# A stack of graph layers on one Trainium2 core: other filler at the start, other closing norms at the end

## The chip, the cores and the metric

The kernel runs on one core of a Trainium2 chip. A core has TensorE (PE in the profile: matrix products and transposes, written to PSUM, eight banks of 128 x 512 f32), VectorE (DVE), ScalarE (ACT), GpSimd (POOL) and SyncE (SP), which issues most DMAs. Each engine works through its own list in order; semaphores order the engines among each other. The metric is the device time of one execution in microseconds, the median of several.

## What is computed

x is 64 batches of 256 nodes with 128 channels, adj is one 256 x 256 matrix for all batches. Four layers follow, each of the form x = layernorm(x + layer(x)):

```python
def layer0(x): # X_k = adj^k x, k = 1..3, the same adj given twice
    return concat([x, X1, X2, X3, X1, X2, X3]) @ weight_1
def layer1(x): return adj @ (x @ weight) + bias
def layer2(x): # A_hat = adj + I, d = rowsum(A_hat)^-0.5
    return (d[:, None] * A_hat * d[None, :]) @ x @ W.T + b
def layer3(h): # five steps
    m = adj @ h                      # in_matrix and out_matrix are both adj
    av = concat([m, m])
    u3 = h @ u3_w.T + u3_b
    z = sigmoid(av @ w3_w.T + w3_b + u3)
    r = sigmoid(av @ w4_w.T + w4_b + u3)
    hv = tanh(av @ w5_w.T + w5_b + (r * h) @ u5_w.T + u5_b)
    h = (1 - z) * h + z * hv
```

The last norm is that of y + h, where y is the input of layer 3 and h its state after five steps.

## The kernel before

Everything is f32. The 64 batches are cut into 32 groups of two (NB = 2); a group is a tile of 128 x 512, four blocks (q) of 128 columns. `Group.record` (L879) doesn't issue instructions: it records operations with their engine, an estimated cost and lag, and what they read and write. `Plan.attempt` (L102) is a list scheduler: it takes, over all engines, the operation that can start earliest by the estimates; among operations that can start equally early on an engine it prefers those that open no new PSUM bank, then the lower `place`, which is the group's rank with a random addition. `Plan.order` (L85) makes 12 such attempts and keeps the one with the shortest estimated end. The instructions are then issued in the order of the estimated starts. So a changed estimate changes the order of the instructions on every engine, the DMA queue of SP among them, but no estimate makes anything wait: only data, buffers and the order on each engine do.

Groups from G - LEVEL = 25 on share nearly one rank, so they advance side by side. A group may start when the group twelve before it has ended (ACTIVE); the load of x of a group from the fifth on waits for the first operation of the group two before it (`load_gate`, L975).

**Start.** PE runs WARM = 12 transposes of `ident` into a spare bank (`warming`, L268). `turned_early` (L285) transposes adj into the bank `p_at` (four transposes) and adds four more idle ones; `halved` (L290) copies the bank to `aT`, one half by ScalarE, one by VectorE. `square` (L297) forms adj times adj in the bank `p_a2`, followed by two idle transposes, and `halved` copies it to `a2T`. VectorE then makes sums of blocks (`block_sums`, L380) and the summed, centred weights of layer 0 (`w0_sums` and `centre`, L312 to L327, from `w0_raw`, loaded at L308). The first three groups (HEAD) turn their x on PE (`transposes`, L815, the bank `ptx`) and multiply it by a2T directly (`pmq`); later groups have x turned by VectorE (`tx`, L889) with a trip through DRAM (`dx`, `xT`), and propagate with seven block products in place of eight (`seven`, L742). The estimates for the loads of the first four groups stand at L881.

**Middle.** A norm of layers 0 to 2 is `spread_of` (L539: ScalarE squares with a running sum, four blocks one after the other as one planned operation; GpSimd raises to the power -0.5) and a scaling on ScalarE (`normalise_centred`). The weights are centred beforehand, so that the mean is zero. In layer 3 a step is `propagate`, two gates from the bank `pr` and the bank `ph`, and VectorE's d = hv - h, e = z d, h + e. The state is kept transposed (`hT`) and brought into natural layout for the next step through DRAM.

**End.** For groups before B - END (29 of them) the last h goes through DRAM into natural layout (`hn`), is added to y, and is normalised from statistics (`statistics`, `normalise`). The last three groups (END = 6 batches) use `closing` (L706): ScalarE copies hT in another order (`hc`); PE adds, in one bank `s3`, hc turned and centred by `less` (identity minus 1/128), y by a product with `ident`, and, when it is there, e turned and centred. Then comes `spread_of`, or for the very last group `spread_at_once` (L555: the statistics by VectorE instead), a scaling by VectorE and one store.

The costs and lags of the estimates are in ns; `pe`, `dve` and `act` (L501 to L508) add the lag to hand over.

## Time and profile before

| | us |
|---|---|
| median of three runs (lowest, highest) | 1335.65 (1334.96, 1336.24) |
| the profiled execution | 1335.43 |
| its span | 1333.5 |
| PE busy | 1321.0 |
| VectorE busy | 1037.3 |
| ScalarE busy | 774.3 |
| GpSimd busy | 632.7 |

The span is the time from the first to the last instruction that the profiler saw on the core; the profiled execution's own time is 1.9 us longer. Busy times of the engines overlap each other. PE and PEld are the products and the loading of their stationary operand. In the page's groups, `s<-less,hc 128*128 128x128` names the tile written, the stationary and the moving operand, and their shapes; every f32 product shows two records, a transpose one. DMA lines of SP show the issue; the landing is told apart. Idle time in brackets behind an instruction is that of its engine just before it, with what ended it.

The rows of the page that cost most are the gates' products on PE:

```profile
L219 PE MATMUL pr<-mg,w435u5T 128*128 128x512 f32 x640 | 321.9, 593 | 0.0
...
L219 PE MATMUL ph<-mg,w435u5T 128*128 128x512 f32 x320 | 163.4, 593 | 0.0
L219 PE MATMUL pr<-hT,w2u3T 128*128 128x512 f32 x320 | 163.0, 592 | 0.0
L219 PE MATMUL ph<-rh,w435u5T 128*128 128x512 f32 x320 | 162.7, 592 | 0.0
```

They run beside each other's loading and overlap by their modelled ends, so that 593 ns of one is more than the spacing of two.

### The profile page before, as it was taken

The page shows a single profiled execution, that of the slowest core. Times are in us where ns is not written, and L with a number is a line of the kernel's source. Part 1 is how long each engine was busy: PE and PEld are TensorE (multiplying, and loading weights), DVE is VectorE, ACT ScalarE, POOL GpSimd, SP SyncE. Part 2 cuts the span into 40 slices and gives each one's busy share as a digit, 9 for nine tenths or more (in the row PEclk, how much of TensorE's full clock was granted, in tenths as well). Part 3 has the DMA queues.
Part 4 walks back from the last instruction along what each step waited for, and adds up shares of the span by engine and source line. Part 5 has one row for each costly group of instructions (what it writes and reads, how often), then busy time and mean ns, then how long its engine had stood idle before and what let it go on. Part 6 is the DMA issues. An engine that isn't in the chain of part 4 may idle for free.

```text
span 1333.5 us, 23248 instructions
## 1 busy us (share of the span) xinstructions
PE 1321.0 (99%) x6901; PEld 925.1 (69%) x6901; DVE 1037.3 (78%) x2574; ACT 774.3 (58%) x2355; POOL 632.7 (47%) x995
## 2 busy tenths in 40 slices
PE   9899999999999999999999999999999999999997
PEld 8887766766666677768677666667677786566554
DVE  6866677978788788796787788878877688777777
ACT  4576654566464664655566655645565787444445
POOL 4885642545352654455446633523444675222212
PEclk9999999999999999999999999999999999999999
DMA  7411343634454444332432443635342134344433
GB/s 185 122 53 43 82 93 90 154 91 107 115 127 111 104 118 105 102 97 73 103 98 78 111 119 106 145 83 125 81 103 64 45 106 116 92 111 93 91 86 103
DMA packets 403276, 134.38 MB, mean 101 GB/s; under 512 B 309808, under 2 KB 374960, under 8 KB 403152
## 3 DMA queue, kind: packets, MB, share of 16 engines
q1 hardware_dynamic: 402896, 132.78, 39.5%
q8 instruction: 55, 0.90, 0.3%
q0 software_dynamic: 256, 0.13, 0.2%
q14 instruction: 69, 0.57, 0.1%
HBM read 67.05 MB, written 65.54 MB: 99 GB/s over the span
## 4 chain that ended last, share of the span: by engine, by line
PE 96%; DVE 3%; DMA 1%; ACT 0%; issue 0%; POOL 0%; POOLq 0%; DVEq 0%; ACTq 0%; SPq 0%
PE pr L219 31%; PE ph L219 20%; PE pmg L219 19%; PE py L219 11%; PE pm L219 7%; PE pz L219 4%; PE pmq L219 3%; DMA x<-in_x_dram 1%; PE s L219 1%; DVE tx L890 0%; PE warm L270 0%; ACT y L545 0%; DVE se L660 0%; DVE sf L663 0%; DVE sd L654 0%
## 5 line engine op out<-in xcount | busy, mean ns | idle before, releaser
L219 PE MATMUL pr<-mg,w435u5T 128*128 128x512 f32 x640 | 321.9, 593 | 0.0
L763 POOL TENSOR_TENSOR tsg<-h 128x256 f32<-128x256 f32 x128 | 94.0, 735 | 286.9 <-DMA h<-dh 195.0
L549 POOL TENSOR_TENSOR rs<-ve,half 128x4 f32<-128x4 f32 x98 | 101.1, 1031 | 170.0 <-ACT y L545 167.5
L869 ACT ACTIVATE pr<-pr,bsum 128x512 f32<-128x512 f32 x160 | 105.5, 659 | 125.1 <-PE pr L219 124.8
L876 DVE TENSOR_TENSOR d<-ph,hT 128x512 f32<-128x512 f32 x160 | 109.6, 686 | 79.4 <-ACT ph L869 73.9
L869 ACT ACTIVATE r<-pr,bsum 128x512 f32<-128x512 f32 x160 | 105.3, 658 | 108.3 <-PE pr L219 100.0
L545 ACT ACTIVATE y<-s,root 128x128 f32<-128x128 f32 x392 | 152.2, 391 | 24.1 <-DVE s L584 22.1
L219 PE MATMUL ph<-mg,w435u5T 128*128 128x512 f32 x320 | 163.4, 593 | 0.0
L219 PE MATMUL pr<-hT,w2u3T 128*128 128x512 f32 x320 | 163.0, 592 | 0.0
L219 PE MATMUL ph<-rh,w435u5T 128*128 128x512 f32 x320 | 162.7, 592 | 0.0
L219 PEld LDWEIGHTS pr<-mg,w435u5T 128*128 128x128 f32 x640 | 107.7, 191 | 63.5 <-issue 47.9
L869 ACT ACTIVATE ph<-ph,bsum 128x512 f32<-128x512 f32 x160 | 105.3, 659 | 72.3 <-PE ph L219 71.7
L876 DVE TENSOR_TENSOR rh<-r,hT 128x512 f32<-128x512 f32 x160 | 109.2, 683 | 30.8 <-ACT r L869 29.6
L219 PEld LDWEIGHTS pmg<-aTp,h 128*128 128x128 f32 x512 | 86.7, 191 | 60.7 <-issue 38.4
L577 ACT ACTIVATE y<-s,rs 128x128 f32<-128x128 f32 x384 | 122.1, 393 | 7.1 <-POOL rs L549 6.9
L876 DVE TENSOR_TENSOR pr<-pr,d 128x512 f32<-128x512 f32 x157 | 108.2, 691 | 1.1
L876 DVE TENSOR_TENSOR hT<-hT,pr 128x512 f32<-128x512 f32 x157 | 106.2, 678 | 1.8
L219 PE MATMUL pmg<-s_aTp,tsg 128*128 128x128 f32 x768 | 106.7, 275 | 0.0
L910 POOL TENSOR_TENSOR yb<-y,wb 128x512 f32<-128x512 f32 x64 | 82.4, 1288 | 41.1 <-ACT y L577 40.8
L219 PEld LDWEIGHTS ph<-rh,w435u5T 128*128 128x128 f32 x320 | 58.0, 190 | 57.6 <-issue 45.6
L219 PEld LDWEIGHTS pmg<-s_aTp,tsg 128*128 128x128 f32 x768 | 96.0, 192 | 0.0
L219 PE MATMUL pmg<-aTp,h 128*128 128x128 f32 x512 | 95.7, 274 | 0.0
(206 smaller groups left out, 2784.7 us busy)
## 6 DMA issues: line engine op xcount, KB each, us to landing
dh<-th SPq DMA_DIRECT2D x160, 256.0 KB, 2.1
h<-dh SPq DMA_DIRECT2D x512, 64.0 KB, 2.4
x<-in_x_dram SPq DMA_DIRECT2D x32, 256.0 KB, 3.2
hT<-dh SPq DMA_DIRECT2D x128, 64.0 KB, 2.0
out_dram<-y SPq DMA_DIRECT2D x32, 256.0 KB, 2.4
dx<-tx SPq DMA_DIRECT2D x29, 256.0 KB, 2.4
xT<-dx SPq DMA_DIRECT2D x58, 128.0 KB, 2.7
dn<-tn SPq DMA_DIRECT2D x29, 256.0 KB, 2.0
```

The lines of the kernel that those rows point to most:

```text
L219: nc.tensor.matmul(o, lhsT, rhs, start=start, stop=stop, skip_group_check=shared)
L545: nc.scalar.activation(nat(y)[:, q, :], nat(s)[:, q, :], AF.Square, scale=C ** -0.5, bias=root[:, 0:1], accum_out=ve.ap[:, q:q + 1])
L549: nc.gpsimd.tensor_tensor(rs.ap, ve.ap, half[:, :self.q], op=OP.pow)
L577: nc.scalar.mul(nat(y)[:, q, :], nat(s)[:, q, :], rs.ap[:, q:q + 1])
L763: nc.gpsimd.tensor_tensor(ts.ap[:, :2 * P].rearrange("p (x c) -> p x c", x=2), ins(h)[:, 1], ins(h)[:, :, 0], op=OP.subtract)
L869: self.act(lambda: nc.scalar.activation(t.ap, ps.ap, func, bias=bias[1], scale=1.0), [ps, bias[0]], [t], act_cost(self.width) + 100)
L876: self.dve(lambda: nc.vector.tensor_tensor(out(t), way(a), way(b), op=op), [a, b], [t])
L910: nc.gpsimd.tensor_tensor(nat(yb), nat(y), bias[1][:, None, :].to_broadcast([P, self.q, C]), op=OP.add)
```

## The change

- **Warming.** The 12 + 4 + 2 idle transposes go. WARM = 7 products of a zeroed tile `blank` take the place of the first 12; nothing takes the place of the others.
- **A^T in two banks.** `p_at` and `p_a2` become two banks each, with two planned operations on PE each, and each half is copied from its own bank.
- **Estimates of the loads.** x of the first three groups is believed to land sooner (2600, 4600 and 7500 ns of lag instead of 6000, 9000 and 10500); `w0_raw` gets the rank -0.4 instead of -1 and so goes to SP behind x of the second group, with 7000 instead of 7300.
- **Pieces.** For the last eight groups (FINE = 8, in groups) the squares of `spread_of` and the last scaling `normalise` are planned block by block instead of four at once.
- **Closing.** END = 8 batches: four groups. `hc` is now VectorE's sum of hT and of hT0, the transposed y from the beginning of layer 3, so that the product of y with `ident` goes.
- **The last two groups** (TAIL = 2): the last tanh, d and e are made by halves (`stepped`), and the closing stands in two banks of two blocks. In `ended`, ScalarE takes squares of the first half, VectorE statistics of the second; one power serves both; ScalarE scales block 0, VectorE blocks 2 and 3 and then block 1; each half has its own store. Val objects `h0`, `h1`, `e0`, `e1` only carry the order; `held` keeps buffers from being given away.

```diff
-END = 6
+TAIL = 2
+FINE = 8
+END = 8
 STEPS = 5
-WARM = 12
+WARM = 7
...
+    blank = const.tile([P, P], F32, name="blank")
+    nc.vector.memset(blank, 0.0)
...
     def warmed():
-        warming(WARM)
-    def warming(n):
-        for i in range(n):
-            nc.tensor.transpose(warm.ap[:, (i % 4) * P:(i % 4 + 1) * P], ident, ident)
+        for i in range(WARM):
+            mm(warm.ap[:, (i % 4) * P:(i % 4 + 1) * P], blank, blank, True, True)
...
-    p_at, p_a2, p_an = temp("p_at"), temp("p_a2"), temp("p_an")
+    p_at, p_a2 = ([temp(f"{name}{mt}") for mt in range(T)] for name in ("p_at", "p_a2"))
+    p_an = temp("p_an")
...
-    def turned_early():
-        turn(p_at, a_nat)
-        warming(4)
-    pre(-8, "PE", 8 * 110, turned_early, [a_nat], [p_at, warm])
+    def turned_early(mt):
+        for nt in range(T):
+            nc.tensor.transpose(p_at[mt].ap[:, nt * P:(nt + 1) * P], a_nat.ap[:, nt, mt * P:(mt + 1) * P], ident)
+    def square(mt):
+        for kt in range(T):
+            mm(p_a2[mt].ap[:, :N], a_nat.ap[:, kt, mt * P:(mt + 1) * P], aT.ap[:, kt, :], kt == 0, kt == T - 1)
     def halved(v, ps):
-        pre(-8, "ACT", act_cost(N), lambda: nc.scalar.copy(v.ap[:, 0, :], ps.ap[:, :N]), [ps], [v], joint=True)
-        pre(-8, "DVE", 420, lambda: nc.vector.tensor_copy(v.ap[:, 1, :], ps.ap[:, N:]), [ps], [v], joint=True)
+        pre(-8, "ACT", act_cost(N), lambda: nc.scalar.copy(v.ap[:, 0, :], ps[0].ap[:, :N]), [ps[0]], [v], joint=True)
+        pre(-8, "DVE", 420, lambda: nc.vector.tensor_copy(v.ap[:, 1, :], ps[1].ap[:, :N]), [ps[1]], [v], joint=True)
+    for mt in range(T):
+        pre(-8, "PE", 440, lambda mt=mt: turned_early(mt), [a_nat], [p_at[mt]])
     halved(aT, p_at)
-    def square():
-        for mt in range(T):
-            for kt in range(T):
-                mm(p_a2.ap[:, mt * N:(mt + 1) * N], a_nat.ap[:, kt, mt * P:(mt + 1) * P], aT.ap[:, kt, :],
-                   kt == 0, kt == T - 1)
-        warming(2)
-    pre(-8, "PE", pe_cost(N, 4) + 220, square, [a_nat, aT], [p_a2, warm])
+    for mt in range(T):
+        pre(-8, "PE", 870, lambda mt=mt: square(mt), [a_nat, aT], [p_a2[mt]])
     halved(a2T, p_a2)
-    w0_raw = load(-1, "w0_raw", [P, C, K0], w0, lag=7300)
+    w0_raw = load(-0.4, "w0_raw", [P, C, K0], w0, lag=7000)
...
+        def pieces(self):
+            n = self.q if self.start < B - FINE * NB else 1
+            return [range(q, q + n) for q in range(0, self.q, n)]
...
-            def squares():
-                for q in range(self.q):
+            def squares(part=range(self.q)):
+                for q in part:
                     nc.scalar.activation(nat(y)[:, q, :], nat(s)[:, q, :], AF.Square, scale=C ** -0.5,
                                          bias=root[:, 0:1], accum_out=ve.ap[:, q:q + 1])
...
-            self.act(squares, [s], [y, ve], 390 * self.q)
+            for part in self.pieces():
+                self.act(partial(squares, part), [s], [y, ve], 390 * len(part), True)
...
+        def ended(self, s):
+            y, st, mv, ve, rs = (self.val(k, n + "3") for k, n in (
+                ("w", "y"), ("st", "st"), ("mv", "mv"), ("ve", "ve"), ("rs", "rs")))
+            halves = [range(t * self.q // 2, (t + 1) * self.q // 2) for t in range(2)]
+            def place(q):
+                t, i = divmod(q, self.q // 2)
+                return s[t].ap[:, i * P:(i + 1) * P]
+            def squares():
+                for q in halves[0]:
+                    nc.scalar.activation(nat(y)[:, q, :], place(q), AF.Square, scale=C ** -0.5,
+                                         bias=root[:, 0:1], accum_out=ve.ap[:, q:q + 1])
             def stats():
-                for q in range(self.q):
-                    nc.vector.bn_stats(st.ap[:, q * 6:(q + 1) * 6], nat(s)[:, q, :])
-                for q in range(self.q):
+                for q in halves[1]:
+                    nc.vector.bn_stats(st.ap[:, q * 6:(q + 1) * 6], place(q))
+                for q in halves[1]:
                     nc.vector.bn_aggr(mv.ap[:, 2 * q:2 * q + 2], st.ap[:, q * 6:(q + 1) * 6])
-                nc.vector.tensor_scalar(ve.ap, mv.ap.rearrange("p (q k) -> p k q", k=2)[:, 1], EPS, None, op0=OP.add)
-            self.dve(stats, [s], [st, mv, ve], 260 * self.q + 110)
+                q = halves[1]
+                nc.vector.tensor_scalar(ve.ap[:, q.start:q.stop], mv.ap.rearrange("p (q k) -> p k q", k=2)[:, 1, q.start:q.stop],
+                                        EPS, None, op0=OP.add)
+            def scaled(t, first):
+                q, n = halves[t], self.q // 2
+                lo = q.start + first
+                nc.vector.tensor_tensor(nat(y)[:, lo:q.stop, :], s[t].ap[:, first * P:n * P].rearrange("p (q c) -> p q c", c=C),
+                                        rs.ap[:, lo:q.stop, None].to_broadcast([P, n - first, C]), op=OP.mult)
+            self.act(squares, [s[0]], [y, ve], 390 * self.q // 2, True)
+            self.dve(stats, [s[1]], [st, mv, ve], 260 * self.q // 2 + 110, True)
             self.add("POOL", 1040, 100, lambda: nc.gpsimd.tensor_tensor(rs.ap, ve.ap, half[:, :self.q], op=OP.pow),
                      [ve], [rs])
-            return y, rs
+            h0, h1 = Val("const", [P, 1], "y0"), Val("const", [P, 1], "y1")
+            h0.tile = h1.tile = root
+            self.act(lambda: nc.scalar.mul(nat(y)[:, 0, :], place(0), rs.ap[:, 0:1]), [s[0], rs, y], [h0], 390)
+            self.dve(lambda: scaled(1, 0), [s[1], rs, y], [h1], 380)
+            self.dve(lambda: scaled(0, 1), [s[0], rs, y, h0], [h0], 230)
+            for t, h in ((1, h1), (0, h0)):
+                q = halves[t]
+                self.add("SP", 450, 2400, lambda q=q: nc.sync.dma_start(self.view(out)[:, q.start:q.stop], nat(y)[:, q.start:q.stop]),
+                         [y, h], [])
...
-            self.act(run, [s, mv, rs], [y], 390 * self.q)
+            for part in self.pieces():
+                self.act(partial(run, part), [s, mv, rs], [y], 390 * len(part), True)
...
-        def closing(self, y, hT, e, behind):
-            s, hc = self.val("bank", "s3"), self.val("w", "hc")
+        def closing(self, first, hT, e, behind):
+            banks = 2 if self.start >= B - TAIL * NB else 1
+            s, hc = [self.val("bank", f"s3{t}") for t in range(banks)], self.val("w", "hc")
             way, out_ = self.by_tile
-            self.act(lambda: nc.scalar.copy(out_(hc), way(hT)), [hT], [hc])
-            def turned(v, start, stop):
-                for q in range(self.q):
-                    mm(s.ap[:, q * P:(q + 1) * P], v.ap[:, q * P:(q + 1) * P], less.ap, start and q == 0, stop, shared=True)
-            def early():
-                turned(hc, True, False)
-                mm(s.ap, ident, y.ap, False, False, shared=True)
-            self.pe(pe_cost(P, self.q) + pe_cost(self.width), early, [hc, y, less], [s], behind=(behind,))
-            self.pe(pe_cost(P, self.q), lambda: turned(e, False, True), [e, less], [s])
-            o, rs = (self.spread_at_once if self.start >= B - NB else self.spread_of)("3", s)
-            self.dve(lambda: nc.vector.tensor_tensor(nat(o), nat(s), rs.ap[:, :, None].to_broadcast([P, self.q, C]),
-                                                     op=OP.mult), [s, rs], [o])
-            return o
+            self.dve(lambda: nc.vector.tensor_add(out_(hc), way(hT), way(first)), [hT, first], [hc])
+            def turned(v, start, stop, t):
+                n = self.q // banks
+                for i in range(n):
+                    q = t * n + i
+                    mm(s[t].ap[:, i * P:(i + 1) * P], v.ap[:, q * P:(q + 1) * P], less.ap, start and i == 0, stop, shared=True)
+            e, part = e if banks == 2 else (e, [e])
+            for v, start, after in ((hc, True, (behind,)), (e, False, ())):
+                for t in range(banks):
+                    op = self.pe(pe_cost(P, self.q // banks), lambda v=v, start=start, t=t: turned(v, start, not start, t),
+                                 [v if start else part[t], less], [s[t]], behind=after)
+                    if v not in op.vals:
+                        self.held(op, v)
+            if banks == 2:
+                return self.ended(s)
+            o, rs = self.spread_of("3", s[0])
+            self.dve(lambda: nc.vector.tensor_tensor(nat(o), nat(s[0]), rs.ap[:, :, None].to_broadcast([P, self.q, C]),
+                                                     op=OP.mult), [s[0], rs], [o])
+            self.add("SP", 450, 2700, lambda: nc.sync.dma_start(self.view(out), nat(o)), [o], [])
...
+        def stepped(self, ph, z, hT):
+            hv, d, e = (self.val("w", name) for name in ("hv", "d", "e"))
+            way, out_ = self.by_tile
+            n = self.q // 2
+            halves = [slice(t * n, (t + 1) * n) for t in range(2)]
+            part = [Val("const", [P, 1], f"e{t}") for t in range(2)]
+            for t, q in enumerate(halves):
+                part[t].tile = root
+                self.act(lambda q=q: nc.scalar.activation(way(hv)[:, q], way(ph)[:, q], AF.Tanh, bias=hb[1], scale=1.0),
+                         [ph, hb[0]], [hv, part[t]], 420, True)
+            for t, q in enumerate(halves):
+                self.held(self.dve(lambda q=q: nc.vector.tensor_tensor(way(d)[:, q], way(hv)[:, q], way(hT)[:, q], op=OP.subtract),
+                                   [part[t], hT], [d, part[t]], 340, True), hv)
+                self.held(self.dve(lambda q=q: nc.vector.tensor_tensor(out_(e)[:, q], way(z)[:, q], way(d)[:, q], op=OP.mult),
+                                   [part[t], z], [e, part[t]], 340, True), d)
+            return e, part
+        def held(self, op, v):
+            op.vals.append(v)
+            v.users.append(op)
...
-            plan.add("SP", 450, dict(zip(range(0, 4 * NB, NB), (6000, 9000, 10500, 9000))).get(self.start, 2700), self.rank() - 1.5, lambda: nc.sync.dma_start(nat(x_), self.view(x)), [], [x_],
+            plan.add("SP", 450, dict(zip(range(0, 4 * NB, NB), (2600, 4600, 7500, 9000))).get(self.start, 2700), self.rank() - 1.5, lambda: nc.sync.dma_start(nat(x_), self.view(x)), [], [x_],
...
-            ats, ins = aT, None
+            hT0, ats, ins = hT, aT, None
...
+                if s == STEPS - 1 and self.start >= B - TAIL * NB:
+                    e = self.stepped(ph, z, hT)
+                    break
...
-                o = self.closing(y, hT, e, gated)
-                self.add("SP", 450, 2700, lambda: nc.sync.dma_start(self.view(out), nat(o)), [o], [])
+                self.closing(hT0, hT, e, gated)
```

More of the change, by code (lines that the diff above doesn't have):

```diff
@@ L1 @@
 import random
+from functools import partial
 from contextlib import ExitStack
@@ L549, in scales @@
                 nc.gpsimd.tensor_tensor(rs.ap, ve.ap, half[:, :self.q], op=OP.pow)
-            self.act(squares, [s], [y, ve], 390 * self.q)
+            for part in self.pieces():
+                self.act(partial(squares, part), [s], [y, ve], 390 * len(part), True)
             self.add("POOL", 1040, 100, scales, [ve], [rs])
             return y, rs
-        def spread_at_once(self, tag, s):
-            st, mv, ve, rs, y = (self.val(k, n + tag) for k, n in (
-                ("st", "st"), ("mv", "mv"), ("ve", "ve"), ("rs", "rs"), ("w", "y")))
+        def ended(self, s):
[9 more added lines that the diff above has]
+                                         bias=root[:, 0:1], accum_out=ve.ap[:, q:q + 1])
@@ L593, in normalise, with run @@
             y = self.val("w", "y" + tag)
-            def run():
-                for q in range(self.q):
+            def run(part):
+                for q in part:
                     nc.scalar.activation(nat(y)[:, q, :], nat(s)[:, q, :], AF.Identity, bias=mv.ap[:, q:q + 1],
                                          scale=rs.ap[:, q:q + 1])
-            self.act(run, [s, mv, rs], [y], 390 * self.q)
+            for part in self.pieces():
+                self.act(partial(run, part), [s, mv, rs], [y], 390 * len(part), True)
             return y
@@ L704, in inner_seven @@
             return s0
-        def closing(self, y, hT, e, behind):
-            s, hc = self.val("bank", "s3"), self.val("w", "hc")
+        def closing(self, first, hT, e, behind):
+            banks = 2 if self.start >= B - TAIL * NB else 1
+            s, hc = [self.val("bank", f"s3{t}") for t in range(banks)], self.val("w", "hc")
             way, out_ = self.by_tile
-            self.act(lambda: nc.scalar.copy(out_(hc), way(hT)), [hT], [hc])
-            def turned(v, start, stop):
-                for q in range(self.q):
-                    mm(s.ap[:, q * P:(q + 1) * P], v.ap[:, q * P:(q + 1) * P], less.ap, start and q == 0, stop, shared=True)
-            def early():
-                turned(hc, True, False)
-                mm(s.ap, ident, y.ap, False, False, shared=True)
-            self.pe(pe_cost(P, self.q) + pe_cost(self.width), early, [hc, y, less], [s], behind=(behind,))
-            self.pe(pe_cost(P, self.q), lambda: turned(e, False, True), [e, less], [s])
-            o, rs = (self.spread_at_once if self.start >= B - NB else self.spread_of)("3", s)
-            self.dve(lambda: nc.vector.tensor_tensor(nat(o), nat(s), rs.ap[:, :, None].to_broadcast([P, self.q, C]),
-                                                     op=OP.mult), [s, rs], [o])
-            return o
```

## The prediction

> **What bounds the kernel.** I read the page's busy shares first, then the chain of waits, then the timelines of both ends.
>
> ```profile
> PE 1321.0 (99%) x6901; PEld 925.1 (69%) x6901; DVE 1037.3 (78%) x2574; ACT 774.3 (58%) x2355; POOL 632.7 (47%) x995
> ...
> PE 96%; DVE 3%; DMA 1%; ACT 0%; issue 0%; POOL 0%; POOLq 0%; DVEq 0%; ACTq 0%; SPq 0%
> ```
>
> TensorE is the bound. A busy share can flatter it, so I priced its records at their spacing when packed: 0.43 us for 512 columns (pr x4 takes 1.72), 0.2155 for 256, 0.111 for 128. For each stretch of 100 us from 100 to 1200 the counts times these prices give 99.6 to 100.4 us. The middle has no slack: an order that keeps TensorE fed costs and gains nothing there, and the time is **head loss + TensorE's work + tail**. From 0 to 30 us the priced work is 25.6 us and from 30 to 60 also 25.6: 8.8 us are lost in the head, beside 18 warming transposes. The PE timeline of the head:
>
> ```profile
> 1.37 2.82 PE L270 MATMUL warm<-ident 128*128 128x128 f32 x12 [1.37 <-POOL ident masks.py:199]
> 3.98 1.06 PE L282 MATMUL p_at<-ident,a_nat 128*128 128x128 f32 x4
> 4.84 1.06 PE L270 MATMUL warm<-ident 128*128 128x128 f32 x4
> 5.69 2.13 PE L219 MATMUL p_a<-aT,a_nat 128*128 128x256 f32 x8
> 7.66 0.38 PE L270 MATMUL warm<-ident 128*128 128x128 f32 x2
> 7.88 0.60 PE L820 MATMUL ptx<-ident,x 128*128 128x128 f32 x4
> ```
>
> To see: start, length, operation. Warming fills the waits for a_nat (issued at 0.75, landing after 2.9), for the copies to aT and for those to a2T. Group 0's x, issued at 1.24 and landing after 3.2, is there at 4.44, yet is turned at 7.88. The chain of waits further on, then TensorE's idle stretch by windows (length, PE busy, PEld, DVE, ACT, POOL, clock, DMA share, GB/s):
>
> ```profile
> 20.94 0.39 DVE sd L654
> 21.32 0.04 SPq L893
> 21.37 0.04 issue
> 21.41 4.11 DMA x<-in_x_dram
> 25.52 0.02 issue
> 25.54 2.10 DVE tx L890 x2
> ```
>
> ```profile
> 34.00:36.00 2.00, 0.94 (x9) 0.75 (x7) 1.97 (x5) 0.78 (x5) 2.00 (x3) 1.00 0.86 263
> 36.00:38.00 2.00, 0.78 (x5) 0.59 (x5) 2.00 (x8) 1.25 (x6) 2.00 (x4) 1.00 0.99 282
> ...
> 42.00:44.00 2.00, 1.16 (x11) 0.99 (x10) 2.00 (x9) 1.80 (x9) 0.54 (x2) 1.00 0.99 277
> ```
>
> VectorE, full from 34 to 44, starves TensorE; but from 22 to 34 it sat waiting 5.9 us for loads of x. Loads of groups 4 and later are gated on the first operation of the group two before; group 4's on group 2's transposes, which ran only at 21.39 (ptx). Two loads were issued at 21.41 and about 22.0; the second is group 4's. The tail:
>
> ```profile
> 1324.68 1.95 PE L219 MATMUL s<-less,e 128*128 128x128 f32 x16
> 1326.66 0.89 DVE L562 BATCH_NORM_STATS2 st<-s 128x6 f32<-128x128 f32 x4 [2.02 <-PE s L219]
> 1327.35 1.01 POOL L549 TENSOR_TENSOR rs<-ve,half 128x4 f32<-128x4 f32 x1 [3.50 <-ACT y L545]
> 1328.33 1.01 POOL L568 TENSOR_TENSOR rs<-ve,half 128x4 f32<-128x4 f32 x1
> 1329.37 0.69 DVE L723 TENSOR_TENSOR y<-s,rs 128x512 f32<-128x512 f32 x1 [0.28 <-POOL rs L568]
> ```
>
> Two groups finish together: statistics, power, scaling, store. TensorE's last work ends at 1324.68 + 16 x 0.111 = 1326.46; 7.04 us follow.
>
> **Front.** Removed: 18 transposes, 2.82 + 0.85 + 0.22 = 3.89 us on the path, and PE's wait of 0.42 for w0s at 12.47. Added: seven f32 matmuls on zeros. A 128-column f32 matmul is two records (24 records of s<-less,e for 12 matmuls), so 14 records. Here a record takes 0.213 to 0.235 us, as long as the cold transposes: 3.0 to 3.3 us. They wait for a VectorE memset (as first operation there, from 0.82, about 0.2 by the 0.22 of a 128-column tensor_scalar) instead of GpSimd's ident at 1.37, so start near 1.05, 0.3 earlier, and end near 4.2, as before. Two PSUM banks let VectorE copy its half of aT as soon as its transposes end; before, it began at 5.49, only when ScalarE's copy ended at 5.45. So aT is ready at about 5.6 instead of 5.91, and ptx of group 0 (0.85 cold) fills that wait. ptx of group 1 fills the a2T wait. Group 2's ptx and pmq, 0.44 + 1.72 = 2.16 us, can run before w0s is ready, provided its load (landed near 9.7) is believed early enough; its due time drops by 3 us. Net: -3.89 - 0.42 - 0.3 + 3.15 + 0.4 (group 0's four transposes cold, 0.85 against 0.44) = **-1.1 us**.
>
> A rule against this: the Trainium skill, "TensorE: Matmul & The Clock Gate", Parts 1 and 4, has the clock rise after some 3.4 us of sustained activity, and transposes not counted as such. The row comes first: warming and p_at transposes are 0.21 to 0.235 apart, packed ones after 7.9 us 0.11, and the eight p_a records (1.97 from start to start against 1.72 packed) mean full rate from about 6.1, only 0.4 us after the first true matmul at 5.69. The granted clock reads 1.00 throughout, so only spacing shows it. By the row the rate rises some 4.7 us after the first PE instruction, now at 5.8: my sum. By the rule, true matmuls from 1.05 lift it near 4.5, saving another 0.9 (p_at and ptx 0.43 each); read against the change, ptx between p_at and the squares breaks activity, and p_a stays cold, +1.7. Both stay as ends; I take **-1.2**.
>
> On SP, w0_raw (448 KB) moves behind x of group 1. Same bytes before it as before group 1's x, which landed at 9.0; so w0_raw near 9.0 instead of 8.15. VectorE reaches it at about 9.5 (s_a2T first), before at 9.80: nothing, with 0.5 in hand. The rest on SP (weights, aTp) keeps its order. Nothing is added on POOL.
>
> **The gap at 35 to 51 us.** With ptx of group 2 near 12 instead of 21.4, group 4's load leaves up to 9 us earlier and its tx can fill VectorE's idle 22 to 34. PE's idle after 34 sums to 1.88 + 0.40 + 0.84 + 0.21 = 3.3 us. Ends: -3.3; nothing, or a worse gap, because group 2's 2.16 us no longer stand as cover. I take **-1.8**, just over half, since some 10 us of late VectorE work can move into 5.9 us of waits but the order is chosen anew.
>
> **TensorE's work.** The matmul adding y (two records of 0.43) goes from three groups: -2.58. A fourth group takes the closing: eight matmuls, 16 x 0.111 = +1.78. **-0.80**. Its store-turn-load-statistics leave VectorE, SP, POOL; hc becomes a VectorE add (0.68) for ScalarE's copy (0.62), beside matmuls, as VectorE is 78% busy. Single-piece squares and normalises (last eight groups) change no work: ScalarE is 58% busy, and a gate waits at most one piece of 0.4 us instead of 1.5.
>
> **Tail.** After the last half: two bn_stats, two aggregates, one add (1.38 for four; half of 1.21 plus 0.17) 0.78, power 1.01, scaling of two tiles 0.42, a third 0.2, and as before 3.44 from VectorE's end (1330.06) to the end; hand-overs 0.15, matmul end 0.15: 6.15 us. The halves' ScalarE work (two squares 0.7, one mul 0.36) lies beside; the two extra store issues (0.35 each) lie ahead of the last. PE waits for tanh, d, e: by halves (0.37 + 0.42 + 0.42, then 0.34 + 0.34 for the second) about 2.15 us from its last u5T matmul; other groups' hc and e, 0.89 each, and the first half cover it. The y matmuls, 1.72 of the cover before, are gone; uncovered it costs up to 1.7. I take 0.15: 6.3 - 7.04 = **-0.75**.
>
> **Sum:** -1.2 - 1.8 - 0.8 - 0.75 = -4.55 us against the profiled 1335.43: 1330.9. The median lies 0.22 above: **1331.1**.
>
> **Rivals.** 0.2%, about what a measurement tells from no change, is 2.7 us: 1333.0 and 1338.3.
> - Forecast, 0.50, own range 1329.3 to 1333.1.
> - *Everything closes*, 0.22: clock up at 4.5 (-2.0), gap gone (-3.3), work and tail: -6.85, 1328.8. For: PE has no other losses early. Against: VectorE is full from 34 on.
> - *The gap takes the front back*, 0.18: the chain of loads and transposes, not PE, rules up to 43 us, so front work done sooner only lengthens the gap. Leaves -1.55: 1334.1. For: the chain holds no PE piece between 20 and 43. The same if the planner doesn't place ptx early. Against: that chain hangs on ptx of group 2.
> - *One more landing at VectorE's head*, 0.10: shorter due times make the plan put a tx before its load lands; VectorE is in order, and sd, us and the copies for PE queue behind. Price: one landing of x, 4.3 us, front eaten: +4.3 - 1.55 = +2.75, 1338.4. It decides once the added wait at VectorE exceeds 1.55 us beyond PE's cover. For: three such waits stand there now. Against: due times were long only for the first loads.
>
> Faster: 0.48 + 0.22 + 0.02 = 0.72; same 0.02 + 0.15 + 0.02 = 0.19; slower 0.09. Range 1327.8 to 1336.5, leaving out about 0.05 below and 0.11 above.
>
> **What would show it.** Front: ptx between p_at and p_a, the second ptx before pmq, group 2's pmq before the first py, which starts near 14. Gap: group 4's load before 15 us, waits of tx under 3 us, PE idle from 34 to 51 under 2. Work: no s<-y,ident; 32 records each of hc and e. Tail: 6.3 us from the last e record to the end. The forecast is wrong if PE idles in the middle, or if p_a's records stay 0.43 apart.

## The result and the profile after

| | before | after |
|---|---|---|
| median (lowest to highest) of six executions each, side by side, us | 1335.95 (1334.96 to 1336.98) | 1330.57 (1329.47 to 1331.35) |
| ratio, 95% interval | | 0.9958 (0.9947 to 0.9968) |
| profiled execution, its span, us | 1335.43, 1333.5 | 1330.67, 1328.9 |

The change makes the kernel faster by 0.42%; the forecast of 1331.1 us is 0.5 above the median. The page of the profile after, busy shares and the chain of waits:

```profile
PE 1319.2 (99%) x6907; PEld 925.0 (70%) x6907; DVE 1038.5 (78%) x2574; ACT 771.5 (58%) x2360; POOL 630.7 (47%) x994
...
PE 99%; DVE 1%; issue 0%; ACT 0%; POOLq 0%; DVEq 0%; ACTq 0%
```

TensorE now carries 99% of the chain instead of 96%. Its timeline at the start (start, length, operation):

```profile
4.21 0.77 PE L290 MATMUL p_at<-ident,a_nat 128*128 128x128 f32 x4
4.82 0.60 PE L863 MATMUL ptx<-ident,x 128*128 128x128 f32 x4
5.44 1.99 PE L222 MATMUL p_a<-aT,a_nat 128*128 128x256 f32 x8
7.27 0.60 PE L863 MATMUL ptx<-ident,x 128*128 128x128 f32 x4
7.71 5.34 PE L222 MATMUL pmq<-a2T,x 128*128 128x256 f32 x24
```

Both ptx stand where the warming stood, and 24 pmq records (three groups) run ahead of the first py; before, it were 16. That py starts at 12.89 us in both kernels, with 1.72 us more work done. The stretch from 30 to 45 us by windows, first before, then after (columns as in the prediction):

```profile
30.00:45.00 15.00, 11.88 (x93) 11.03 (x92) 14.18 (x36) 8.66 (x36) 10.63 (x16) 1.00 0.91 246
```

```profile
30.00:45.00 15.00, 14.65 (x115) 13.90 (x114) 14.85 (x34) 8.57 (x37) 12.33 (x18) 1.00 0.88 234
```

TensorE's second number rises from 11.88 to 14.65: the gap is nearly gone, though VectorE (fourth number) is as full as before. The tail after:

```profile
1321.41 1.06 PE L222 MATMUL s<-less,e 128*128 128x128 f32 x8
...
1322.50 0.49 DVE L580 BATCH_NORM_STATS2 st<-s 128x6 f32<-128x128 f32 x2 [0.68 <-PE s L222]
...
1323.56 1.01 POOL L595 TENSOR_TENSOR rs<-ve,half 128x4 f32<-128x4 f32 x1 [0.59 <-DVE ve L584]
...
1324.60 0.69 DVE L590 TENSOR_TENSOR y<-s,rs 128x256 f32<-128x256 f32 x2 [0.65 <-POOL rs L595]
```

TensorE ends at 1321.41 + 8 x 0.111 = 1322.30; 6.6 us follow, 7.04 before.

The table splits every profiled span by the method of the prediction: the length of a stretch minus the records in it at their packed spacing, warming counted as lost. A record missing from a trace shifts such a number by 0.1 to 0.4. "Tail" runs from the end of the last e records to the end of the span.

| kernel | median us (n) | ratio to before | span | lost to 60 us | lost 300 to 600 | lost 900 to 1100 | tail |
|---|---|---|---|---|---|---|---|
| before | 1335.95 (6) | 1 | 1333.5 | 10.7 | 1.0 | 0.3 | 7.0 |
| after | 1330.57 (6) | 0.9958 (0.9947, 0.9968) | 1328.9 | 5.4 | 3.0 | 0.4 | 6.6 |
| a1_turns | 1329.81 (1) | | 1328.0 | 6.6 | 1.2 | 0.3 | 6.6 |
| a3_one_bank | 1331.61 (1) | | 1329.7 | 7.1 | 2.4 | 0.5 | 6.4 |
| a4_x_late | 1332.90 (1) | | 1331.1 | 8.1 | 2.6 | -0.2 | 6.6 |
| b1_anT_late | 1332.37 (10) | 0.9972 (0.9962, 0.9981) | 1328.2 | 7.4 | 0.9 | -0.1 | 6.7 |
| b2_anT_early | 1338.30 (12) | 1.0013 (1.0004, 1.0021) | 1336.0 | 12.5 | 1.4 | 0.9 | 7.0 |
| c1_apart | 1330.44 (4) | 0.9954 (0.9939, 0.9968) | 1328.1 | 5.4 | 2.9 | 0.3 | 6.6 |
| c2_plan0 | 1337.05 (12) | 1.0004 (0.9996, 1.0013) | 1333.8 | 8.4 | 0.3 | 4.5 | 6.4 |
| d1_no_halves | 1331.50 (5) | 0.9970 (0.9952, 0.9989) | 1327.2 | 5.4 | 0.5 | -0.1 | 7.2 |
| d2_three | 1328.92 (4) | 0.9947 (0.9932, 0.9962) | 1326.4 | 6.1 | 0.7 | 0.4 | 6.4 |
| d3_whole | 1335.59 (12) | 0.9999 (0.9991, 1.0008) | 1334.1 | 6.2 | 2.8 | 3.0 | 6.9 |
| e1_front | 1331.02 (5) | 0.9963 (0.9950, 0.9976) | 1329.2 | 5.7 | 0.1 | 1.4 | 7.1 |
| e2_tail | 1331.93 (6) | 0.9969 (0.9957, 0.9981) | 1330.7 | 9.4 | 0.9 | -0.2 | 6.3 |

From before to after: head -5.3 (of it -1.6 up to the first py), TensorE's work -0.8, a new stall between 300 and 600 us +2.0, tail -0.4. Together -4.5, of the 4.6 us between the spans. The median of the kernel before was 1336.83, 1336.28 and 1336.27 beside the later runs, so kernels of different batches are compared by ratio.

### The profile page after: what moved, and what is told of

Its sections match the earlier page's. It is cut to its first block, busy times and chain, and to the rows that moved or that the text cites. A ratio compares the mean times of both kernels' runs of the same rounds, so it can differ in the third digit from the quotient of the medians.

```text
span 1328.9 us, 23277 instructions
## 1 busy us (share of the span) xinstructions
PE 1319.2 (99%) x6907; PEld 925.0 (70%) x6907; DVE 1038.5 (78%) x2574; ACT 771.5 (58%) x2360; POOL 630.7 (47%) x994
## 4 chain that ended last, share of the span: by engine, by line
PE 99%; DVE 1%; issue 0%; ACT 0%; POOLq 0%; DVEq 0%; ACTq 0%
PE pr L222 31%; PE ph L222 21%; PE pmg L222 19%; PE py L222 12%; PE pm L222 7%; PE pz L222 4%; PE pmq L222 4%; PE s L222 1%; PE warm L222 0%; PE p_a L222 0%; DVE se L696 0%; DVE s L624 0%; PE ptx L863 0%; DVE sf L699 0%; POOLq L1092 0%
```

## The experiments

### The start: what fills it

**a1_turns** puts idle transposes back in place of the products of zeros.

```diff
-        for i in range(WARM):
-            mm(warm.ap[:, (i % 4) * P:(i % 4 + 1) * P], blank, blank, True, True)
+        for i in range(13):
+            nc.tensor.transpose(warm.ap[:, (i % 4) * P:(i % 4 + 1) * P], ident, ident)
```

> The changed kernel, its order of instructions kept, with 13 transposes of ident in place of the seven products on zeros (13 so that they end near 4.4 us as well, although ident is ready 0.3 us later). Theory 'products raise the clock': transposes do not count as activity, so p_at's four transposes stand 0.21 apart (0.85 us in the chain instead of 0.56), those of group 0's x likewise (0.85 instead of 0.44), full speed comes near 6 us, and the first py starts 0.7 to 1.0 us later than at 13.05. Theory 'time since the first instruction', which my prediction used: nothing moves by more than 0.1 us.

Measured: p_at and ptx stayed at 0.21 us a record, and the first py came at 13.44 instead of 12.89. That looks like proof that products raise TensorE's rate and transposes do not. It does not stand. Eight kernels here, the changed one among them, have the same TensorE instructions up to p_a, and their rates rose at different times. TensorE in c1_apart, then in d3_whole, both after seven products of zeros:

```profile
4.10 0.60 PE L290 MATMUL p_at<-ident,a_nat 128*128 128x128 f32 x4
```

```profile
4.21 1.06 PE L291 MATMUL p_at<-ident,a_nat 128*128 128x128 f32 x4
...
5.92 2.27 PE L223 MATMUL p_a<-aT,a_nat 128*128 128x256 f32 x8
```

In c1_apart the four transposes are fast from the first (0.60 with a modelled end of some 0.16 in it); in d3_whole even two of the eight p_a records are still slow (2.27 against 1.89 packed), so the rate rose near 6.7. The traces tell it directly. Each keeps a record of the granted clock, which begins, at full rate, at 3.97 us in c1_apart and at 4.54, 5.13, 5.19, 5.60, 5.64, 6.40 and 6.68 in the other seven; the profile's rows read 1.00 ahead of that only because nothing is on record there. After transposes the record begins at 4.73 (b2_anT_early), 6.17 (before), 6.27 (a1_turns) and 7.18 (e2_tail). So a1_turns, with its first py at 13.44, stands between e1_front (5.64, py at 13.14) and d2_three (6.40, py at 13.51): its delay is that of its late rise. And in b2_anT_early the rate rose at 4.73, before the first true product (p_a at 5.41): transposes were enough.

The records also show what the moment hangs on. In all 14 traces the full rate lasts a whole number of stretches of 3.413 us (386 to 388 of them; 10 and 378 in b2_anT_early). It begins at the end of the first such stretch that TensorE filled to 0.85 or more; where a stretch was filled to 0.80 or less, the rate did not rise. Where these stretches lie against the start of the kernel differs from execution to execution, so the same start can rise one stretch sooner or later, and no gain of products over transposes shows. The Trainium skill, "TensorE: Matmul & The Clock Gate", Part 1, has an activity window of some 3.4 us that runs free of the kernel's start. The spread of 2.7 us for one and the same start fits that; it doesn't fit the 0.5 us either way that the same part gives for the rise.

**a3_one_bank** keeps all of the change but puts both halves of adj and both of its square in one bank again.

```diff
-            nc.tensor.transpose(p_at[mt].ap[:, nt * P:(nt + 1) * P], ...
+            nc.tensor.transpose(p_at[1].ap[:, mt * N + nt * P:mt * N + (nt + 1) * P], ...
...
-            mm(p_a2[mt].ap[:, :N], ...
+            mm(p_a2[0].ap[:, mt * N:(mt + 1) * N], ...
```

> The changed kernel, order kept, with both halves of A^T in one bank and both halves of its square in one bank. Theory 'a bank serves one engine at a time': the second copy of each pair starts only when the first has ended, and the first copy of the square waits for all of its products: aT ready 0.35 us later, a2T 0.4 later still, the first py at about 13.8 instead of 13.05. Theory 'the copies wait for each other because they write one SBUF tile': no change, 13.05.

Measured: VectorE's copy of aT ran from 5.26, ScalarE's only from 5.72, one behind the other, and so again for a2T (8.17 and 8.57). TensorE waited 0.48 for aT, and the first py came at 13.91. That is later than in any of the eight kernels with the unaltered start. In b1_anT_late and d1_no_halves, whose rate rose at almost the same time (5.19 and 5.13; here 5.04), it came at 13.18. So the copies side by side are worth 0.73 us in this one execution, as this run's first theory had it (13.8 against 13.05); the prediction had counted 0.3, for aT alone.

**a4_x_late** moves the turning of group 0's x, and its copy, behind the squares: in the finished order, `moved(ops, [53, 54], 8)` puts operations 53 (PE ptx) and 54 (ACT xT) directly behind operation 8 (PE p_a).

> The changed kernel with the transposes of group 0's x, and the copy behind them, moved behind the square of adj, everything else in its order. Theory 'the x transposes fill the wait for aT': PE idles about 0.7 us instead of 0.26 before the square, and the first py comes 0.44 us later, at 13.5. Rival, that the wait for a2T behind the square has room for them: 13.05.

Measured: first py at 15.12. Two things come together. ScalarE, in order, copied xT (8.92) ahead of its half of a2T, for which TensorE then waited 0.51. And the p_a records took 2.71 against 1.89 packed, after an idle 0.46. The clock record shows why: the rate rose at 7.22, since the stretch that ended at 3.81 was filled to only 0.80. The idle time came later and didn't keep the rate low: the next stretch, with the idle time in it, was filled to 0.86 and was enough. The late rise is the smaller part. Against d3_whole (6.68, py at 13.65) the first py is 1.47 later, and 0.54 us more at half rate cost 0.27.

### The gap: why VectorE no longer starves TensorE

The forecast hung the gap on group 4's load, to leave some 9 us earlier. It did not. SP in the changed kernel:

```profile
20.57 0.33 SPq L960 DMA_DIRECT2D dx<-tx  x1
20.94 1.05 SPq L948 DMA_DIRECT2D x<-in_x_dram  x2
```

The two loads left at 20.94 and 21.42, half a microsecond sooner than before (21.41 and 21.89), and ahead of ptx of group 2, which ran from 21.96. Before, too, both left before that ptx had ended (21.60 to 22.20). So neither waited for it: `load_gate` orders the plan, and on the chip the loads stand in SP's queue behind a dx<-tx, which waits for VectorE's tx (19.44 to 20.54). What moved is VectorE's work on anT and s_anT, from 31 to 36 us to 23.4 to 25.4, into its wait for x. Some lines of it, first before, then after:

```profile
31.27 0.82 DVE L368 TENSOR_SCALAR anT<-p_an,dinv 128x256 f32<-128x256 f32 x2
...
33.71 1.13 DVE L385 TENSOR_TENSOR s_anT<-anT 128x128 f32<-128x128 f32 x1
34.87 0.70 DVE L386 TENSOR_TENSOR s_anT<-s_anT,anT 128x128 f32<-128x128 f32 x1
```

```profile
23.37 0.88 DVE L369 TENSOR_SCALAR anT<-p_an,dinv 128x256 f32<-128x256 f32 x2 [1.47 <-PE p_an L285]
24.28 0.29 DVE L386 TENSOR_TENSOR s_anT<-anT 128x128 f32<-128x128 f32 x1
```

Before, the two additions shown also ran beside GpSimd's (33.39 to 35.42) and took 1.13 and 0.70 instead of 0.29. VectorE's waits for x between 22 and 34 us fell from 5.86 us to nothing. **b1_anT_late** undoes just that move in the changed kernel (`moved(ops, [20], 1943)`, `moved(ops, [23], 1292)`: anT behind tx of group 9, s_anT behind tx of group 6).

> The changed kernel with two operations of VectorE moved back to where the kernel before had them: the scaling of anT behind the third of the transpositions tx that begin at 25 us, its block sums behind the fourth; everything else in its order. Theory 'VectorE's order closed the gap': PE idles 2 to 3 us more between 30 and 50 us and the kernel is 2 to 3 us slower, at 1333. Theory 'the load of group 4' (my prediction): that load leaves at the same time as before, so nothing changes, 1330.6.

Measured: 0.9972 against 0.9958, some 1.9 us, with intervals that just overlap, and 2.0 more lost to 60 us. Of this, 1.5 lies between 30 and 60 us, where the kernel before loses 4.7, the changed one 1.0 and this one 2.5. (Its profiled execution, which had no stall near 380 us, was the shortest of its ten.) VectorE again waited 3.13 for x, and TensorE 1.37 for mq at 37.6. So some two fifths of the gap are that order. **b2_anT_early** is the reverse: in the kernel before, p_an, anT and s_anT go into the wait (`moved(ops, [17, 18, 21], 444)`).

> The kernel before, with three operations moved forward: the transposes for anT on PE to behind the transposes and products of group 2's x, its scaling and its block sums on VectorE to in front of the transpositions tx that begin at 25 us; everything else, the loads too, in its order. Theory 'VectorE's order made the gap': the 3 us of VectorE work run in the wait for the loads, PE's idle time between 30 and 50 us falls from 3.3 us to 1 to 2, and the kernel is 1.5 to 2.5 us faster than before. Theory 'the load of group 4': same as before.

A miss: slower than before, by 1.7 us by the ratio. VectorE and GpSimd in b2_anT_early:

```profile
25.80 0.29 DVE L386 TENSOR_TENSOR s_anT<-s_anT,anT 128x128 f32<-128x128 f32 x1
26.01 1.37 DVE L387 TENSOR_TENSOR s_anT<-anT 128x128 f32<-128x128 f32 x1
27.30 0.81 DVE L388 TENSOR_TENSOR s_anT<-anT,s_anT 128x128 f32<-128x128 f32 x1
...
28.17 2.08 DVE L890 STREAM_TRANSPOSE tx<-x 128x512 f32<-128x512 f32 x2
```

```profile
25.97 1.26 POOL L910 TENSOR_TENSOR yb<-y,wb 128x512 f32<-128x512 f32 x1 [1.44 <-ACT y L577]
27.20 0.77 POOL L763 TENSOR_TENSOR ts<-y 128x256 f32<-128x256 f32 x1
```

An addition of 0.29 takes 1.37 while GpSimd adds, and 0.81 behind its next one. The tx pair starts at 28.17 instead of 25.54, and the next two loads leave 2.6 us later (29.67 instead of 27.08 for the first). In the changed kernel the same five operations were done at 25.4, before GpSimd began at 25.78. But in this profiled execution the granted clock fell as well (last but two of the numbers):

```profile
38.00:40.00 2.00, 1.79 (x11) 1.79 (x12) 1.13 (x4) 1.12 (x4) 2.00 (x4) 0.72 1.04 320
40.00:42.00 2.00, 2.00 (x10) 1.82 (x10) 2.00 (x5) 0.42 (x2) 1.87 (x3) 0.50 0.72 162
42.00:44.00 2.00, 2.00 (x19) 2.00 (x19) 2.00 (x7) 0.96 (x5) 1.44 (x4) 0.93 0.91 270
```

From 38.86 to 42.27 it was 0.50, after a stretch of 3.41 us in which TensorE was busy for 0.40 of the time. The records in these 3.41 us are worth 1.67 at their packed spacing, so the slow clock cost about 1.75 us, nearly all of the added loss to 60 us (12.5 instead of 10.7). It is not the whole cause: the eight executions with a mean clock of 0.999 are no faster than the four with 0.997 or 0.998 (medians 1338.4 and 1337.8). So what makes this order slower in every execution stays open; the profile shows only that the wait was filled at the price of a later tx.

**e1_front** takes all edits of the start, the loads' estimates among them, into the kernel before, and leaves its end alone. **e2_tail** takes all edits of the end and leaves the start.

```diff
 e1_front: WARM = 7, blank, two banks, lags 2600, 4600, 7500, w0_raw at -0.4; END = 6 and the old closing
 e2_tail:  TAIL = 2, FINE = 8, END = 8, closing with the first h; WARM = 12, one bank, the old lags
```

> The changes of the start alone (products for warming, two banks, estimates of the loads), the end as in the kernel before; the planner draws its order anew and believes the end 2.0 us sooner than for the kernel before. 'The start brings the head's whole 5.5 us': first py about 1.5 us sooner, loss from 0 to 60 us near 5.6, time about 5 us under the kernel before. 'The order drawn for the whole kernel decides': the planner now has 1.7 us of TensorE's idle time near 1000 us, so about 3.5 us under the kernel before. My forecast's parts would give 3.0 (1.2 + 1.8). If the loss from 0 to 60 us stays above 9, the start does not reach past the first py.

> The changes of the end alone (fourth closing, hc with the first h, halves in the last two groups, pieces), the start as in the kernel before. 'A sum of parts': TensorE's work -0.8 and the tail -0.4 to -0.75, so 1.2 to 1.5 us under the kernel before. 'The order drawn decides': the planner, which has all the draws to make anew, believes the end 2.1 us less idle in the first 60 us, so 3 to 4 us under the kernel before, with the loss from 0 to 60 us at 9 instead of 11.1. If the tail measures 7 us or more with the halves, they bring nothing.

Measured: e1_front loses 5.7 to 60 us, like the changed kernel: the edits of the start, in the order drawn for them, close the gap. It gives 1.1 back near 1086 us, as expected of its own order, and its tail is the old 7.1. e2_tail, whose start is unedited, loses 9.4, although its first py came 1.05 later than in the kernel before (its rate rose at 7.18 instead of 6.17). Between 30 and 60 us it loses 2.5 instead of 4.7: with the old start, a new draw alone took 2.2 of the gap's 3.7. It measures 0.9969, some 4.1 us by the ratio but 2.8 by the spans; its profiled execution is the slowest of its six. By the spans, start and end give -4.3 and -2.8; that is 7.1 together, in which 1.3 of the head is counted twice. The changed kernel has 4.6. Between stand the stall of 2.0, which neither half has, and e1_front's own 1.1, which the changed kernel doesn't have; 0.3 remain. By the ratios it is 4.9 and 4.1 against 5.6. Which edit of the start closes the gap was not split further.

### The order drawn

The planner's own estimate ranks twelve drawn orders. For the changed kernel the tenth is the best, and nine of the twelve have 3 to 6 us of idle TensorE between 1000 and 1100 us. **c2_plan0** keeps the change to the letter and takes the first draw, without random additions, which was the best one for the kernel before.

```diff
+        drawn = [[0.0] * 7029] + [[rng.random() for _ in range(7029)] for _ in range(tries - 1)]
+        for t in (0,):
```

> The changed kernel, not one operation different, in the order of the planner's first attempt, without random additions, instead of its tenth. The planner believes this order to be 6.8 us longer, with 6.2 us of idle PE near 1000 us. Theory 'the order drawn is part of the gain': the idle time shows near 1000 us and the kernel takes 1335 to 1337, no faster than before. Theory 'any order that feeds PE is as good', as I predicted: 1330.6.

Measured: 1.0004, the whole gain gone. It loses 3.0 more in the head and 4.1 more between 900 and 1100. Two of TensorE's waits there:

```profile
1084.41 0.71 PE L223 MATMUL pmg<-s_aTp,tsg 128*128 128x128 f32 x4 [0.75 <-POOL tsg L807]
...
1090.13 0.46 PE L223 MATMUL pmg<-s_aTp,h 128*128 128x128 f32 x2 [0.84 <-ACT m L854]
```

That is where the last seven groups begin to advance side by side. "An order that keeps TensorE fed costs and gains nothing" is true; that the new order would feed it was assumed.

This run also has what the forecast wanted for the gap, and the gap stays. Here ptx of group 2 ran at 11.39, and two loads of x left at 12.01 and 13.69 (in the changed kernel at 13.47 and 20.94). Yet it loses 3.7 us between 30 and 60, where the changed kernel loses 1.0 and the kernel before 4.7.

### The new stall in the middle

VectorE, GpSimd and TensorE of the changed kernel near 380 us:

```profile
378.00 1.80 DVE L624 TENSOR_TENSOR s<-hn,y 128x512 f32<-128x512 f32 x1
379.72 1.48 DVE L696 TENSOR_TENSOR se<-ss,xT 128x256 f32<-128x256 f32 x1
```

```profile
377.96 2.95 POOL L977 TENSOR_TENSOR yb<-y,wb 128x512 f32<-128x512 f32 x2
```

```profile
381.59 1.12 PE L222 MATMUL pr<-mg,w435u5T 128*128 128x512 f32 x2 [1.42 <-DVE mg L842]
```

s<-hn,y has a median of 0.68 over its 28 and se one of 0.42; here they take 1.80 and 1.48, while GpSimd makes two additions in a row. se ends 0.3 after the end of GpSimd's pair (380.91), and in a1_turns, where GpSimd's first addition stands alone (378.15 to 379.44), s<-hn,y took 1.81 too and ended 0.6 after it. So they wait for all of the other's addition and then run at about their usual length. The rest of this trace agrees. All 16 of the sums sd, ss, se and sf that took over 0.70 began during a GpSimd operation. And rh<-r,hT, as long as s<-hn,y but with r in PSUM, took at most 0.69 in all of its 160, though 49 of them began while GpSimd was adding or subtracting. mg is behind the two additions, and TensorE waits for mg.

The Trainium skill, "SBUF — State Buffer", in "SBUF: two separate sides", says the same: a VectorE operation with two inputs in SBUF and a GpSimd operation that reads SBUF exclude each other for a whole instruction. In a1_turns GpSimd's second addition started 0.59 late, behind ScalarE's y, se took 0.41, and the wait for mg was absent. So it depends on some tenths of a microsecond and differs between executions.

The kernels with the same order there bear this out. Where s<-hn,y and se took 1.80 and 1.48 (the changed kernel, a4_x_late, and d3_whole with 1.81), TensorE idled 1.85 or 1.86 in two waits, 1.42 or 1.43 and then 0.43. Where they took 0.81 or 0.82 and 0.41 (b1_anT_late, d1_no_halves, d2_three), because s<-hn,y began only near the end of GpSimd's addition, it did not wait at all.

**c1_apart** moves the two additions behind mg (`moved(ops, [1285, 3045], 1676)`).

> The changed kernel with two additions of VectorE, both of whose operands lie in SBUF (s<-hn,y of batch 10 and se<-ss,xT of batch 28), moved behind the two mg<-pmg that stood next, so that they no longer stand between PE's products and the two additions yb of GpSimd at 378 us; everything else in its order. Theory 'VectorE waits for GpSimd's end': PE's wait of 1.4 us for mg at 381 us goes in every execution, 0.7 to 1.4 us in the median. Rival, that PE then waits for another operation just behind: no change.

Measured: the wait for mg is gone, and se still takes 1.48 there. But TensorE idles 1.85 once at 384.26, as long as in its two waits before. The view names no releaser; VectorE's mg<-wsg,pmg ends just ahead of it:

```profile
383.88 0.28 DVE L838 TENSOR_TENSOR mg<-wsg,pmg 128x128 f32<-128x128 f32 x1
```

```profile
384.26 0.46 PE L222 MATMUL pmg<-s_aTp,h 128*128 128x128 f32 x2 [1.85 <-issue]
```

The same pair, 0.10 us apart, stands in the changed kernel (384.77 and 384.87). That mg comes behind the two additions and the statistics of s<-hn,y in both orders, so the delay reached TensorE a little later: the run's rival came true. The loss from 300 to 600 is 2.9, as in the changed kernel, and the time the same (0.9954 against 0.9958). That GpSimd prolongs the two additions is shown, and that TensorE's idle time goes with it; that moving them behind two mg gains time is not.

### The end

**d1_no_halves** takes the halves of the last two groups away. Here and in the next two the tenth draw is kept, but it goes by the number of an operation: those recorded behind the first edited one get other random additions (in d1_no_halves in the last two groups, in d2_three in the last four, in d3_whole in the last eight).

```diff
-TAIL = 2
+TAIL = 0
```

> The changed kernel without the halves of the last two groups (TAIL = 0: whole tanh, d and e, one bank, squares on ScalarE for all four blocks, one store); the order is the changed kernel's up to the last groups. Theory 'the halves shorten the last chain': 0.7 for tanh, 0.7 for d and e, 0.7 for the squares, less 0.4 that filler hides: 1.5 to 2 us slower, all of it behind PE's last product or just before it. Rival, other groups' work covers it: within 0.5 us.

Measured: the tail is 7.2. In all kernels with halves it is 6.3 to 6.9, without them 7.0 to 7.2: some 0.5 us, shown. On the whole time it is not settled: the span of 1327.2 equals the changed kernel's less its 1.85 us of idle time near 380 us (1327.05), and by the ratios d1_no_halves is 1.6 us slower, with intervals that overlap. One of its five executions weighs on that: 1337.06, with a mean clock of 0.997. The other four took 1329.01 to 1332.03.

**d2_three** lets only three groups close on TensorE.

```diff
-END = 8
+END = 6
```

> The changed kernel with three groups closing on TensorE instead of four (END = 6), the drawing of the order kept. 'TensorE's work is the time': 16 records fewer, 1.78 us less, so about 1328.8. 'The fourth group's closing is filler where other groups wait for their last tanh, d and e': the 1.8 us come back as idle time of TensorE after 1200 us (the planner has 1.5 there), so 1330.6, the same as the changed kernel.

Measured: 1328.92, 0.9947 (0.9932 to 0.9962). This is the lowest time of the study and the number that "TensorE's work is the time" gave, but its interval overlaps that of the changed kernel. TensorE waits once at the end, for e of the last half:

```profile
1319.13 1.16 PE L223 MATMUL s<-less,e 128*128 128x128 f32 x8 [0.83 <-DVE e L933]
```

So of the 1.78 us saved some 0.8 stands there as a wait: both expectations have a part. The fourth closing brings nothing that was measured; leaving it out may bring 1 to 1.5 us.

**d3_whole** plans squares and scalings of the last eight groups four blocks at once again.

```diff
-FINE = 8
+FINE = 0
```

> The changed kernel with the squares and last scalings of the last eight groups planned four blocks at once again (FINE = 0), the drawing of the order kept. My forecast: nothing, as ScalarE is 58% busy, so 1330.6. 'A gate queued behind 1.5 us of squares keeps TensorE waiting': idle time of TensorE after 900 us, up to the planner's 4.5 us, so 1332 to 1335.

Measured: 0.9999; some 5.5 us, the whole gain. Windows from 1084 to 1098, d3_whole and then the changed kernel:

```profile
1084.00:1098.00 14.00, 12.68 (x87) 10.35 (x86) 11.91 (x31) 13.90 (x58) 8.38 (x12) 1.00 0.33 103
```

```profile
1084.00:1098.00 14.00, 14.00 (x98) 11.59 (x97) 11.07 (x28) 12.30 (x51) 9.81 (x15) 1.00 0.28 95
```

ScalarE, fifth number, is busy 13.90 of 14 us in d3_whole and 12.30 in the changed kernel; its 58% is a mean over the kernel. The wait itself (1.21 at 1097.70) is for VectorE's mg, and another, of 1.11 at 1326.35, for e. Which of ScalarE's pieces holds VectorE up was not followed to its end.

The 5.5 us are not the price of whole pieces alone. The kernel has 6939 operations instead of 7029, and with their numbers all operations behind the first whole piece, those of the last eight groups, got other places in the order. For this order the planner itself expects 2.9 us of idle TensorE between 1000 and 1100 us; over the twelve draws of the same kernel it expects from 0.0 to 5.8. Two kernels with whole pieces and their own best draw lose less between 900 and 1100 than the 3.0 here: e1_front 1.4, the kernel before 0.3. Pieces and redraw were not told apart.

## Why the prediction was right, and where not

The sum was right to 0.5 us by luck, since two errors of about 2 us cancel: the gap closed by 1.9 more than forecast, and a stall of 2.0 came in the middle. In the head it is rather the rival *Everything closes* that came true: its -2.0 and -3.3 against -1.6 and -3.7 measured.

- **Front, -1.2.** Measured -1.6 in the profiled execution; over the seven of the eight that run 24 pmq records on end before py, whose first py has a mean of 13.17 against 13.29 in three kernels with the old start (12.89, 13.05, 13.94), it is -1.7: 1.72 more work done, 0.12 sooner, less 0.16, by which a packed record's start shows too early beside one that follows a wait. The steps held: ptx in the two waits, group 2's pmq ahead of py, copies side by side; only group 2's own ptx did not come early (21.96). The reading of the clock failed in both its forms, by row and by rule. Each took from one execution, or from a fixed 3.4 us, a moment that varies by 2.7 us among eight executions of one start; and b2_anT_early speaks against the part of the rule by which transposes don't count.
- **Gap, -1.8.** The step that failed is "group 4's load leaves up to 9 us earlier". The loads left about when they did before, and they never waited for group 2's transposes, in either kernel. The -3.7 came from VectorE's order: anT and s_anT in the landing wait are worth 1.5 to 1.9 (b1_anT_late). The rest goes with the order drawn: e1_front with the new start has all of it, e2_tail with the old start 2.2, c2_plan0 with the new start but another draw only 1.0.
- **Middle, 0.** Failed by +2.0: the drawn order puts VectorE's additions beside GpSimd's, and 1.85 us of TensorE's idle time are in the trace. By the prediction's own sign ("wrong if PE idles in the middle") this part was wrong. Profiles of three kernels with this order don't have the stall (b1_anT_late, d1_no_halves, d2_three).
- **Work, -0.80.** Held by count: no s<-y,ident, 32 records each of hc and e. That the +1.78 of the fourth closing buys something elsewhere was not claimed, and d2_three shows nothing that it buys.
- **Pieces, 0.** "ScalarE is 58% busy, and a gate waits at most one piece of 0.4 us instead of 1.5": not settled in size. Without the pieces the kernel is 5.5 us slower, but with other places for the last eight groups as well. What failed is the reason: a mean over the kernel was used for a stretch in which ScalarE is busy 12.30 to 13.90 of 14 us.
- **Tail, -0.75.** Measured -0.44; the chain was as listed, and four of its terms were mis-sized. Statistics took 0.92 (1322.50 to 1323.42) for 0.78, scaling 0.69 for 0.62, hand-overs and matmul end 0.37 for 0.30, and from VectorE's end to the end of the span 3.61 for 3.44; only the 0.15 for an uncovered wait wasn't needed, as TensorE was fed up to the last e records. In d2_three and d3_whole that cover fails, by 0.83 and 1.11.

## What to carry to other kernels

Where instructions are put in order by a planner, every edit redraws the whole order, and the redraw can be worth more than the edit: here some 6 us between two draws of one and the same change (1.0004 against 0.9958), against a gain of 5.6. So test an edit under more than one draw, and count what each stretch loses, not only the total. A busy share is read over the stretch in question: an engine at 58% on the whole was busy 13.90 of 14 us where TensorE waited. And what depends on the phase of something outside the kernel, as the rise of the rate at the start does, is not to be read off a single execution.

## What the runs showed of the hardware

- The moment at which TensorE reaches full rate differs between executions of the same first instructions: 3.97 to 6.68 us after the start of the span among eight. In 14 executions it came at the end of the first stretch of 3.413 us that TensorE filled to 0.85 or more, and transposes alone were enough in b2_anT_early (4.73). The profile's rows read 1.00 ahead of it, where no clock is on record.
- In b2_anT_early the granted clock fell to 0.50 for 3.41 us, after a stretch of that length in which TensorE was busy for 0.40 of the time.
- VectorE additions of two SBUF operands wait for a whole GpSimd addition: 1.80 instead of 0.68, 1.48 instead of 0.42, 1.37 instead of 0.29. A product of the same length with one operand in PSUM did not: rh took at most 0.69 in 160.
- Two copies out of one PSUM bank ran one after the other (VectorE from 5.26, ScalarE from 5.72 in a3_one_bank, released by VectorE's copy); out of two banks they overlapped (4.80 to 5.22 and 5.02 to 5.39). Since a semaphore released the second, this shows the order that the program keeps, not what the bank itself would allow.
